# Two-layer graph attention kernel: the last graphs' logits with WX stationary, their Wh evicted in place, the adjacency cast in quarters, masks and small vectors in another order

## The chip, the cores and the metric

The kernel runs on one core of a Trainium2 chip. The metric is the device time of one execution in microseconds (us), start of the program to its end. The engines of a core work side by side and meet at semaphores: TensorE (PE in the profile, with its weight loads as PEld), VectorE (DVE), ScalarE (ACT), GpSimd (POOL) and SyncE (SP, which here only issues transfers). Transfers are issued from SP, ACT and POOL and carried by 16 DMA engines.

## The reference, cut to what matters

Sixteen graphs of 1024 nodes with 256 features pass through two layers. The first layer is the one that the change touches:

```python
Wh = einsum('bnf,of->bno', h, W)
ei, ej = Wh @ a1, Wh @ a2
att = ei[:, :, None] + ej[:, None, :]
att = bn(att, g1, b1)              # over graphs and columns, one mean and variance per row
att = where(att >= 0, att, 0.2 * att)
att = bn(att, g2, b2)
att = softmax(att, axis=2) * adj
h = elu(bn(att @ Wh, g3, b3))
x = layernorm(x + h)
```

The two norms over `att` need the logits `ei` and `ej` of all 16 graphs before any graph can be aggregated. The second layer (four heads of attention over the same adjacency, with residual and layernorm) is the same before and after.

## The kernel before

The first layer runs in three stages, called A, B and C below.

**Stage A (lines 275 to 399)** makes the logits of all graphs. `WX` holds W with ten more columns: two for the logits and eight for the second layer. A graph's x (1 MB) is loaded by SP, five graphs ahead (`XB = 5`). It is worked through in four items of two 128-row blocks. `turn` transposes an item on PE (four matmuls with the identity, line 314), and ACT copies the result to SBUF (line 324). `product` multiplies it with `WX`, the transposed x being the stationary operand (line 338). For the first ten graphs the product has 266 columns. It is evicted by DVE to `wx` (line 343, two buffers), `finish` stores it as `wh_dram` (line 350) and copies the logits out (lines 351 and 352). For the last six graphs (`LATE`), only the ten extra columns are made (`pe`), and the transposed x stays in SBUF in the buffers that will hold masks and Wh later (`room`, `held`). Their Wh is made in stage B.

**Stage B (lines 401 to 656)** computes the two norms' statistics. First comes a chain of small DVE operations with two column sums on PE and one power on POOL (lines 470 to 533), then the thresholds are spread over the partitions (`theta_rows`, line 457). For each graph, a loop then compares 1024 thresholds with eight columns of values (line 610 on DVE, line 614 on ACT), sums by matmul (line 633) and collects (`compared`, line 559). Beside it `late.make` works off the products left over, two or three 128-row blocks per graph (line 423). It evicts them to a `wx` of its own with two buffers (lines 428 and 430) and stores each graph when complete (line 432). SP's queue here carries these stores, the first mask (line 142, a transposing transfer of the bf16 adjacency into SBUF), the broadcast rows `eb` (line 250) and `wh` of graphs 0 and 1 (line 246), in this order of issue:

```python
late.make(2 + (b % 2 == 0), True)
if b == 3:
    mts[0] = mask(mpool, 0, "mt0")
if b == 9:
    queries(0)
    queries(1)
    for n in range(min(2, B)):
        load(n)
```

The second mask follows after the loop, once the held x are used up.

**Stage C (lines 661 to 802)** aggregates. `weights` makes a graph's attention weights in eight slices on ACT and DVE (lines 672 to 686), one graph ahead of PE, and `aggregate` multiplies them with Wh on PE (line 716).

The adjacency comes as f32 and is used as bf16. `Casts.behind` (line 93) has POOL copy one element of a given tile, which makes POOL wait until that tile is written, and then issues a cast of one whole graph from DRAM to DRAM (line 98). Two are released in stage A (behind the logits of graphs 1 and 5), three in the loop of stage B (behind the sums of graphs 1, 6 and 11), the other eleven in stage C.

The order on PE, ACT, DVE and SP is the program's own in stages A and B. In stage C a scheduler sets it, and the transfers that belong to later stages (`shifted1`, lines 201 and 202, which rewrites `W1s` shifted by one row, so that one transfer covers 127 rows) are issued as early as their dependences allow: these two stand in SP's queue right behind the first five loads of x.

Of the kernel before, what the change touches and what calls it, by code (L numbers as in the profile page):

```python
# [19 lines left out]
P = 128  # L20
# [7 lines left out]
def kernel(  # L28
# [57 lines left out]
    class Casts:  # L86


        def __init__(self):
            self.b = 0  # L90
            self.mark = cpool.tile([1, 1], F32, name="mark")

        def behind(self, data):
            if self.b == B:
                return
            tc.keep_in_program_order(nc.gpsimd.tensor_copy(self.mark, data))  # L96
            tc.keep_in_program_order(
                nc.gpsimd.dma_start(
                    adj16[self.b].rearrange("(k p) j -> p k j", p=P),
                    adj[self.b].rearrange("(k p) j -> p k j", p=P),  # L100
                )
            )
            self.b += 1
# [112 lines left out]
    with ExitStack() as l0:  # L216
# [19 lines left out]
        LATE = 6  # L236
        xw = spool.tile([P, K, B, 2 * H], F32, name="xw")
# [14 lines left out]
        def room():  # L252

            held = {}
            late = list(range(B - LATE, B))
            for n, of in enumerate((0, 4)):
# [6 lines left out]
            for n in range(2):  # L263
                t = epool.tile([P, K, F], F32, tag="wh", name=f"held_w{n}", bufs=2)
                held[late[2 + n]] = t.rearrange("p k (c n) -> p k c n", c=C)
# [9 lines left out]
        with tc.tile_pool(name="apool", bufs=1) as apool, tc.tile_pool(  # L275
# [4 lines left out]
            XB = 5  # L280
            KK = 2
            xin, xTs, wxs, pxs, pes = {}, {}, {}, {}, {}
# [5 lines left out]
            w0 = apool.tile([P, C, F], F32, name="w0")  # L288
            nc.scalar.dma_start(w0, W0.rearrange("(c p) f -> p c f", p=P))
# [15 lines left out]
            load_x(0)  # L305
            wbc = load1w(apool)
            for b in range(1, min(XB, B)):
                load_x(b)
# [17 lines left out]
            def product(b, kk):  # L326
                if kk == 0 and b in held:
                    pes[b] = aps_w.tile([P, K, FX - F], F32, tag="w", name=f"pe_{b}")
                elif kk == 0:
                    wxs[b] = apool.tile([P, K, FX], F32, tag="wx", name=f"wx_{b}", bufs=2)  # L330
                for k in range(KK):
                    n = kk * KK + k
                    if b in held:
                        pw, lo = pes[b][:, n], F
                    else:
                        pw, lo = aps_w.tile([P, FX], F32, tag="w", name=f"pw0_{b}_{n}"), 0
                    for fc in range(C):
                        nc.tensor.matmul(  # L338
                            pw, xTs[b, kk][:, k, fc, :], WX[:, fc, lo:FX],
                            start=(fc == 0), stop=(fc == C - 1),  # L340
                        )
                    if b not in held:
                        nc.vector.tensor_copy(wxs[b][:, n, :], pw)

            def finish(b):
# [7 lines left out]
                if b + XB < B:  # L353
                    load_x(b + XB)
                if b in (1, 5):
                    casts.behind(eT[0:1, b, 0, 0:1])
                if b == 1:
                    parameters1()
                if b == 4:
                    parameters1_made()  # L360
# [20 lines left out]
            turn(0, 0)  # L381
            turn(0, 1)
# [3 lines left out]
            items = [(b, kk) for b in range(B) for kk in range(K // KK)]  # L386
            for n, (b, kk) in enumerate(items):
                product(b, kk)
                if kk == K // KK - 1:
                    finish(b)  # L390
                if n + 2 < len(items):
                    turn(*items[n + 2])
                if n == 5:
                    pv = aps.tile([P, P], F32, tag="aps", name="pv_1")
                    nc.tensor.transpose(pv, rows[1], ident)
                    nc.vector.tensor_copy(vecs[:, NA:at], pv[:, NA:at])
            nc.sync.dma_start(
# [3 lines left out]
        with tc.tile_pool(name="bpool", bufs=1) as bpool, tc.tile_pool(  # L401
# [5 lines left out]
            class Late:  # L407


                def __init__(self):  # L410
                    self.n, self.wx = 0, None

                def make(self, count, shared):

                    for _ in range(count):
                        if self.n == LATE * K:
                            return
                        b, k = B - LATE + self.n // K, self.n % K
                        if k == 0:
                            self.wx = bpool.tile([P, K, F], F32, tag="wx", name=f"wx_{b}", bufs=2)  # L420
                        pw = bps_w.tile([P, F], F32, tag="w", name=f"pw0_{b}_{k}")
                        for fc in range(C):
# [3 lines left out]
                            )  # L426
                        if shared and self.n % 2:
                            nc.vector.tensor_copy(self.wx[:, k], pw)
                        else:
                            nc.scalar.copy(self.wx[:, k], pw)  # L430
                        if k == K - 1:
                            nc.sync.dma_start(wh_dram[b], self.wx)
# [102 lines left out]
            ths = {b: theta_rows(b) for b in range(min(NT, B))}  # L535
            to_rows(th_dram, theta.rearrange("p b k -> p (b k)"), "th")
            to_rows(ec_dram, ec.rearrange("p b k -> p (b k)"), "ec")

# [7 lines left out]
            rest = small(qpool, "rest", [B, K])  # L546
            for n, src in ((1, ec), (4, e2)):
                nc.vector.tensor_copy(powers[:, :, :, n], src)
                nc.vector.tensor_tensor(rest, src, powers[:, :, :, n], ALU.subtract)
                nc.vector.tensor_copy(powers[:, :, :, n + 1], rest)  # L550
                nc.vector.tensor_tensor(rest, rest, powers[:, :, :, n + 1], ALU.subtract)
                nc.vector.tensor_copy(powers[:, :, :, n + 2], rest)
            nc.vector.tensor_scalar(
                powers[:, :, KV:, :], powers[:, :, KV:, :], 0.5, None, ALU.mult
            )
# [3 lines left out]
            def compared(b):  # L559
# [7 lines left out]
                if b in (1, 6, 11):  # L567
                    casts.behind(sums[0:1, 0, 0, b : b + 1])

            t1 = small(qpool, "t1", [B])  # L570
            nc.vector.tensor_scalar(t1, p_mean, float(N), None, ALU.mult)
            t2 = small(qpool, "t2", [B])
            nc.vector.tensor_tensor(t2, p_mean, p_mean, ALU.mult)
# [1470 lines left out]
```

## Time and profile before

| | |
|---|---|
| time, median of 3 runs | 2304.25 us (2298.92 to 2311.9) |
| the profiled execution's own time | 2281.53 us |
| its span in the profile | 2279.8 us |
| PE busy | 2065.0 us (91% of the span) |
| DVE busy | 1823.9 us (80%) |
| ACT busy | 1454.4 us (64%) |
| granted TensorE clock, mean | 0.924 of full speed |

The profile shows one execution, 1% shorter than the median of the timed runs. The stages in it: A from 0 to 185 us, B to 313 us, where the first aggregation matmul starts, C to 821 us, the second layer after that. Some groups of instructions with count, busy time and mean duration of one (an fp32 matmul leaves two records, a transpose one):

```profile
L338 PE MATMUL pw<-WX,xT 128*128 128x266 f32 x320 | 82.7, 403 | 19.7 <-DVE wx L343 18.9 <-DVE WX L385 0.8
L314 PE MATMUL px<-ident,x 128*128 128x128 f32 x256 | 49.0, 326 | 0.0
L338 PE MATMUL pe<-WX,held_m 128*128 128x10 f32 x128 | 24.5, 324 | 0.0
L324 ACT COPY held_m<-px 128x512 f32<-128x512 f32 x16 | 9.4, 586 | 25.1 <-PE px L314 25.1
```

A matmul's duration in such a row includes the time in the pipeline, so a stretch of PE work is read from the starts in the timeline, not from these means.

### The profile page before, as it was taken

How to read it: one execution, taken by the hardware profiler on the slowest of the kernel's cores; microseconds unless marked ns; L12 is line 12 of the kernel's file. 1: busy time of each engine (PE TensorE's matmuls, PEld its weight loads, DVE VectorE, ACT ScalarE, POOL GpSimd, SP SyncE). 2: the span in 40 equal slices, each digit the busy share in tenths (PEclk: the TensorE clock that was granted, in tenths of full speed). 3: DMA queues.
4: the chain of work that ended last, by engine and by line, in shares of the span. 5: the costliest groups of instructions: out<-in, count | busy, mean ns of one | idle time of the engine just before them, and what ended most of it. 6: DMA issues, size and time to landing. Idle time of an engine off the chain costs nothing.

```text
span 2279.8 us, 36099 instructions
## 1 busy us (share of the span) xinstructions
PE 2065.0 (91%) x12248; PEld 1625.0 (71%) x12248; DVE 1823.9 (80%) x4468; ACT 1454.4 (64%) x3192; POOL 938.5 (41%) x1019
## 2 busy tenths in 40 slices
PE   5999677999999955999999999999999999999997
PEld 4798543444444423888888888887888888888886
DVE  2416588999999845789789889788898888898786
ACT  1225466777777613767767767767867857767775
POOL 1001000000000004767657667656667667667572
PEclk9967787999999975999999999999999999999998
DMA  7844968999995225756756746756756756756551
GB/s 210 251 162 131 256 141 180 227 223 228 233 237 143 100 84 170 223 163 169 207 154 166 216 157 167 210 156 162 212 165 166 212 162 164 202 175 164 122 160 42
DMA packets 321224, 403.14 MB, mean 177 GB/s; under 512 B 171089, under 2 KB 267397, under 8 KB 310021
## 3 DMA queue, kind: packets, MB, share of 16 engines
q1 hardware_dynamic: 269389, 254.73, 39.2%
q0 software_dynamic: 51072, 145.61, 26.0%
q8 instruction: 99, 1.62, 0.3%
q14 instruction: 96, 0.79, 0.1%
q10 hardware_dynamic: 568, 0.40, 0.1%
HBM read 329.32 MB, written 104.88 MB: 190 GB/s over the span
## 4 chain that ended last, share of the span: by engine, by line
PE 48%; DVE 19%; issue 17%; DMA 7%; POOL 4%; ACT 4%; SPq 1%; DVEq 0%; ACTq 0%; POOLq 0%
PE pa L716 12%; PE pv L1806 11%; PE pt L1783 8%; PE pu L1711 7%; PE po L1414 3%; POOL xc L1489 3%; DMA x<-in_x_dram 3%; PE pw L338 2%; DMA xc<-xe_dram,ix 2%; DVE d L610 2%; PE pz L1584 2%; DVE v L1814 1%; DVE w L1524 1%; DVE B L1375 1%; DVE w L1520 1%
## 5 line engine op out<-in xcount | busy, mean ns | idle before, releaser
L1489 POOL DMA_INDIRECT xc<-xe_dram,ix x640 | 682.5, 1066 | 212.0 <-issue 183.1
L1806 PE MATMUL pv<-W1s,sT 128*128 128x256 f32 x2048 | 506.1, 391 | 0.4 <-ACT sT L1800 0.4
L716 PE MATMUL pa<-em,wh 128*128 128x512 f32 x1024 | 450.5, 598 | 15.6 <-DVE em L680 15.6
L1806 PEld LDWEIGHTS pv<-W1s,sT 128*128 128x128 f32 x2048 | 382.0, 197 | 44.4 <-ACT sT L1800 0.8
L716 PEld LDWEIGHTS pa<-em,wh 128*128 128x128 f32 x1024 | 193.8, 192 | 248.0 <-issue 244.6
L1783 PEld LDWEIGHTS pt<-MX,s 125*128 125x128 f32 x2560 | 349.3, 203 | 29.7 <-ACT sT L1793 8.9
L1783 PE MATMUL pt<-MX,s 125*128 125x100 f32 x2560 | 350.1, 286 | 4.4 <-ACT sT L1793 2.0
L1711 PE MATMUL pu<-xc,w 128*125 128x256 f32 x1280 | 346.6, 390 | 0.5 <-ACT s L1777 0.5
L1820 ACT ACTIVATE m<-v,neg 128x512 f32<-128x512 f32 x256 | 183.7, 718 | 200.4 <-DVE v L1814 145.6
L1777 ACT ACTIVATE s<-pu,z 125x256 f32<-125x256 f32 x640 | 261.5, 474 | 76.2 <-DVE z L1769 50.1
L1711 PEld LDWEIGHTS pu<-xc,w 128*125 128x125 f32 x1280 | 232.3, 192 | 35.1 <-issue 5.7
L1793 ACT COPY sT<-pt 128x500 f32<-128x500 f32 x256 | 144.1, 563 | 111.9 <-PE pt L1783 111.9
L672 ACT ACTIVATE e<-eb,c,s 128x1024 f32<-128x1024 f32 x128 | 153.8, 1234 | 74.0 <-DVE sm L686 26.6
L1863 POOL TENSOR_TENSOR ors<-ors,mhalf 128x1 f32<-128x1 f32 x128 | 113.1, 883 | 207.2 <-DVE ors L1857 205.9
L1814 DVE TENSOR_TENSOR v<-pv,x 128x512 f32<-128x512 f32 x256 | 175.1, 684 | 14.9 <-PE pv L1806 14.5
L676 ACT ACTIVATE e<-e,v,u 128x1024 f32<-128x1024 f32 x128 | 152.6, 1231 | 26.2 <-DVE e L675 22.1
L680 DVE TENSOR_TENSOR em<-e,mt 128x1024 f32<-128x1024 f32 x128 | 155.2, 1221 | 4.6 <-ACT e L676 3.9
L675 DVE SCALAR_TENSOR_TENSOR e<-e 128x1024 f32<-128x1024 f32 x128 | 152.3, 1221 | 3.1 <-ACT e L672 3.1
L1584 PE MATMUL pz<-IW,h 128*128 128x136 f32 x512 | 90.2, 308 | 61.9 <-DVE fs L1601 37.7
L96 POOL COPY mark<-hb 1x1 f32<-1x1 f32 x11 | 2.8, 252 | 332.3 <-DVE sums L731 332.3
L1584 PEld LDWEIGHTS pz<-IW,h 128*128 128x128 f32 x512 | 77.3, 205 | 77.2 <-issue 44.0
L686 DVE TENSOR_TENSOR sm<-sm,e 128x1024 f32<-128x1024 f32 x96 | 117.4, 1223 | 1.2 <-ACT e L676 1.0
(323 smaller groups left out, 3300.0 us busy)
## 6 DMA issues: line engine op xcount, KB each, us to landing
x<-in_x_dram SPq DMA_DIRECT2D x32, 1024.0 KB
adj<-in_adj_dram POOLq DMA_DIRECT2D x16, 2048.0 KB
rw<-adj SPq DMA_DIRECT2D x32, 1024.0 KB
A<-u_dram SPq DMA_DIRECT2D x128, 250.0 KB
xe_dram<-x SPq DMA_DIRECT2D x16, 1060.0 KB
wh_dram<-wx SPq DMA_DIRECT2D x16, 1024.0 KB
wh<-wh_dram SPq DMA_DIRECT2D x16, 1024.0 KB
h_dram<-hb SPq DMA_DIRECT2D x16, 1024.0 KB
```

Source lines behind the costliest of these rows:

```text
L672: nc.scalar.activation(e, ebs[b], AF.Identity, bias=c1[:, k, b : b + 1], scale=s1[:, k : k + 1])
L676: nc.scalar.activation(e, e, AF.Exp, bias=v2[:, k : k + 1], scale=u2[:, k : k + 1])
L680: nc.vector.tensor_tensor(em, e, mts[b][:, k, :], ALU.mult)
L716: nc.tensor.matmul(acc[b, hf, oc].rearrange("p k q -> p q k"), wh[b][:, k, oc * P : (oc + 1) * P], ems[b, k][:, hf * HALF : (hf + 1) * HAL ...
L1489: nc.gpsimd.indirect_dma_start(out=self.xc[:, i, :], out_offset=None, in_=xe_dram[g.b % 2], in_offset=bass.IndirectOffsetOnAxis(ap=g.l.ix[ ...
L1584: nc.tensor.matmul(pz[:, oc, :], self.h[:, oc, k * P : (k + 1) * P], IW[:, oc, :], start=True, stop=True,)
L1711: nc.tensor.matmul(pu[0:QR, 0:F], c.w[:, k].rearrange("p h q -> p (h q)"), c.xc[:, k, 0:F], start=(i == 0), stop=(i == len(OF[q]) - 1),)
L1777: nc.scalar.mul(f.s[0:QR, i], f.pu[i][0:QR, 0:F], f.z[0:QR, i : i + 1])
L1783: nc.tensor.matmul(self.pt[:, :, :, i], self.first.s[0:QR, i, self.hp * P : (self.hp + 1) * P], MX[0:QR], start=True, stop=True,)
L1806: nc.tensor.matmul(self.pv[:, hh, :], self.first.sT[:, fc, self.hp * HP + hh, :], W1s[:, fc, self.hp * HP + hh, :], start=(fc == 0), stop= ...
L1814: nc.vector.tensor_tensor(self.v2, self.pv, self.g.x[:, self.it].unsqueeze(1).to_broadcast([P, HP, F]), ALU.add)
L1820: nc.scalar.activation(self.m, self.v2, AF.Exp, bias=neg1, scale=1.0)
```

## The change

1. **Late graphs' logits.** For the six late graphs `WX`'s ten columns become the stationary operand and 512 rows of transposed x stream past them: four fp32 matmuls per graph (`logits`). DVE copies the 10x512 result to SBUF twice per graph, and eight transposes per graph bring it back to rows (`turned_logits`), two items later.
2. **Order of graphs.** Stage A takes graphs 2 to 15 first and then 0 and 1 (`ORDER`), so the late ones are 12, 13, 14, 15, 0 and 1.
3. **Wh in place.** `late.make` evicts a product over the held x that it came from. There is no `wx` in stage B, graphs 0 and 1 are neither stored nor loaded again, and the held buffers are dealt out otherwise.
4. **`wx` in stage A** has three buffers instead of two.
5. **Casts in quarters.** `Casts.behind` casts 256 rows at a time. Nine quarters are released in stage A (one behind each of the first nine graphs), fifteen in the loop of stage B (one behind each graph's sums), four after graph 0 of stage C and four with each graph after that.
6. **Order in stage B.** Only graph 0's thresholds are spread ahead of the rows' stores. The powers and the moments of z are computed inside the loop. The masks are issued at graphs 4 and 10.
7. In stage A `W0` is loaded behind the small vectors `a1` and `a2`.

```diff
@@ Casts
         def behind(self, data):
-            if self.b == B:
+            b, part = divmod(self.n, 4)
+            if b == B:
                 return
             tc.keep_in_program_order(nc.gpsimd.tensor_copy(self.mark, data))
+            n = N // 4
+            rows = slice(part * n, (part + 1) * n)
             tc.keep_in_program_order(
                 nc.gpsimd.dma_start(
-                    adj16[self.b].rearrange("(k p) j -> p k j", p=P),
-                    adj[self.b].rearrange("(k p) j -> p k j", p=P),
+                    adj16[b][rows].rearrange("(k p) j -> p k j", p=P),
+                    adj[b][rows].rearrange("(k p) j -> p k j", p=P),
                 )
             )
...
+        ORDER = list(range(2, B)) + [0, 1]
...
@@ room
-            late = list(range(B - LATE, B))
-            for n, of in enumerate((0, 4)):
+            late = ORDER[B - LATE :]
+            for n, of in enumerate((0, 2)):
...
-                t = epool.tile([P, K, F], F32, tag="wh", name=f"held_w{n}", bufs=2)
-                held[late[2 + n]] = t.rearrange("p k (c n) -> p k c n", c=C)
+                t = wh[n] = epool.tile([P, K, F], F32, tag="wh", name=f"wh_{n}", bufs=2)
+                held[late[4 + n]] = t.rearrange("p k (c n) -> p k c n", c=C)
...
+            def logits(b, hf):
+                ps = aps_w.tile([OC, HALF], F32, tag="w", name=f"pl0_{b}_{hf}")
+                for fc in range(C):
+                    nc.tensor.matmul(
+                        ps, WX[:, fc, F:FX], held[b][:, hf * KH : (hf + 1) * KH, fc, :],
+                        start=(fc == 0), stop=(fc == C - 1),
+                    )
+                if hf == 0:
+                    els[b] = apool.tile([OC, N], F32, tag="el", name=f"el_{b}", bufs=2)
+                nc.vector.tensor_copy(els[b][:, hf * HALF : (hf + 1) * HALF], ps)
+
+            def turned_logits(b):
+                pe = pes[b] = aps.tile([P, K, OC], F32, tag="aps", name=f"pe_{b}")
+                for k in range(K):
+                    nc.tensor.transpose(
+                        pe[:, k], els[b][:, k * P : (k + 1) * P], ident[0:OC, 0:OC]
+                    )
...
@@ finish
-                if b in (1, 5):
+                if n < 9:
                     casts.behind(eT[0:1, b, 0, 0:1])
...
                 product(b, kk)
-                if kk == K // KK - 1:
-                    finish(b)
+                if b in held and kk % 2 == 1:
+                    logits(b, kk // 2)
+                if kk == KN - 1 and b not in held:
+                    finish(n // KN)
+                before = items[n - 2][0] if n >= 2 else None
+                if before in held and items[n - 2][1] == KN - 1:
+                    turned_logits(before)
+                    finish((n - 2) // KN)
                 if n + 2 < len(items):
                     turn(*items[n + 2])
...
@@ Late.make
+                        to = held[b][:, k].rearrange("p c n -> p (c n)")
                         if shared and self.n % 2:
-                            nc.vector.tensor_copy(self.wx[:, k], pw)
+                            nc.vector.tensor_copy(to, pw)
                         else:
-                            nc.scalar.copy(self.wx[:, k], pw)
-                        if k == K - 1:
-                            nc.sync.dma_start(wh_dram[b], self.wx)
+                            nc.scalar.copy(to, pw)
+                        if k == K - 1 and b > 1:
+                            nc.sync.dma_start(wh_dram[b], held[b].rearrange("p k c n -> p k (c n)"))
...
-            ths = {b: theta_rows(b) for b in range(min(NT, B))}
+            ths = {0: theta_rows(0)}
             to_rows(th_dram, theta.rearrange("p b k -> p (b k)"), "th")
             to_rows(ec_dram, ec.rearrange("p b k -> p (b k)"), "ec")
+            for b in range(1, min(NT, B)):
+                ths[b] = theta_rows(b)
...
-                if b in (1, 6, 11):
+                if b < 15:
                     casts.behind(sums[0:1, 0, 0, b : b + 1])
...
                 late.make(2 + (b % 2 == 0), True)
-                if b == 3:
+                if b == 4:
                     mts[0] = mask(mpool, 0, "mt0")
+                if b == 10:
+                    mts[1] = mask(mpool, 1, "mt0")
                 if b == 9:
                     queries(0)
                     queries(1)
-                    for n in range(min(2, B)):
-                        load(n)
...
@@ stage C
-                    if n == K + 4 and b > 0:
-                        casts.behind(hb[b][0:1, 0, 0:1])
+                    if n % 4 == 3 and b > 0:
+                        casts.behind(ems[b, k][0:1, 0:1])
```

## The prediction

> **What bounds the kernel now.** The page's second part comes first: which engine is full in which fortieth (57 us).
>
> ```profile
> PE   5999677999999955999999999999999999999997
> DVE  2416588999999845789789889788898888898786
> PEclk9967787999999975999999999999999999999998
> ```
>
> From the eighth slice on PE is full at full clock, but for the turn between the layers (slices 15 and 16). The first seven, stages A and B, are not, and all the edits but the cast's pacing lie there. Next, the busy times by window (columns: window, its length, busy PE, PEld, DVE, ACT, POOL, granted clock, DMA share, GB/s):
>
> ```profile
> 40.00:60.00 20.00, 3.61 (x21) 2.85 (x19) 0.00 (x0) 1.17 (x2) 0.61 (x1) 0.69 1.04 255
> 140.00:160.00 20.00, 20.00 (x100) 20.00 (x99) 0.61 (x4) 5.06 (x9) 0.00 (x0) 0.50 0.15 52
> 220.00:240.00 20.00, 19.50 (x371) 17.50 (x370) 20.00 (x47) 17.99 (x22) 4.74 (x7) 1.00 1.09 234
> 240.00:260.00 20.00, 11.19 (x155) 9.09 (x153) 6.42 (x16) 4.82 (x6) 0.08 (x1) 0.72 1.11 204
> 399.00:430.20 31.20, 31.19 (x92) 15.03 (x91) 29.48 (x33) 23.64 (x27) 1.85 (x2) 1.00 1.01 226
> ```
>
> At 40 us all stand and the DMA is full. At 140 PE works, at half clock. At 220 DVE is the bound of stage B's loop. At 240 all stand again. A graph of stage C takes 31.2 us with PE and DMA both full. The chain of waits names the two stalls (start, length, what):
>
> ```profile
> 39.49 0.63 SPq L202
> 40.21 20.30 DMA wh_dram<-wx
> 60.61 0.45 DVE wx L343
> ...
> 254.88 9.76 SPq L142
> 264.76 4.23 DMA wh_dram<-wx
> ```
>
> Both end with a store that frees a `wx` buffer. SP's timeline says why the stores were late:
>
> ```profile
> 19.04 21.08 SPq L202 DMA_DIRECT2D W1s<-in_L_gnn_W_dram  x1
> 219.15 45.49 SPq L142 DMA_TRANSPOSE mt<-adj  x1
> 264.76 0.97 SPq L432 DMA_DIRECT2D wh_dram<-wx  x2
> 265.79 2.35 SPq L250 DMA_DIRECT2D eb<-ec_dram  x2
> ```
>
> SP is held 21 us by a shift of W1s queued behind one that covers 127 rows, and 45 us by a mask; a mask's median over the 16 is 11.2 us.
>
> **Stage A, the stall at 40 us.** PE stops at 43.6, waits 17.6 us (61.19), then runs eight matmuls at half clock (3.73 us for 1.80): 1.9 more. A second wait at 118 costs 1.35. Sum 20.9. With three buffers PE may run one graph further, 8.96 us (four items of 0.44+1.80), to 52.5. But the first two quarters fall into the time in which the 127-row transfer moves 25 GB/s (24 to 40 us), about a sixteenth of the 380 GB/s that the same queue moves at 116 to 124. The Trainium skill, DMA: Bandwidth & Descriptors, "Why a DMA increments its semaphore by 16 and not by 1", says that 127 partitions put a transfer on one engine; the trace agrees. A quarter puts 16 packets of 0.18 us (below) on that engine too, 2.9 us each: SP is freed near 46 instead of 40.2, the store behind it lands near 53 to 55. I keep **3 us** of stall (ends 0 and 6). Afterwards the DMA holds the pace narrowly: 2 MB per graph at 380 GB/s are 5.4 us, a quarter 2.9, sum 8.3 of 8.96. Gain 20.9-3 = **18**.
>
> **Stage A, late graphs.** Before, from 131.6 to 184.9: 53.3 us, half clock from 136.3 on. After, per graph at full clock: 16 transposes at 0.11 = 1.76; the logits' 4 fp32 matmuls of 512 columns, 8 records at 0.43 (stage C's pace: 64 in 27.5 us) = 3.44; eight small transposes, bound by their weight loads as the 128x10 products are (0.10 each at full clock) = 0.8; twice a wait for ACT's copy (0.26 to start, 0.59, 0.05 back, less one turn of 0.44) = 0.92. Together 6.92, six times 41.5, less 0.9 for turns made earlier, plus 2.2 at the end (copy 0.95, eight transposes, two handovers): 42.8. DVE's 12 copies (bounds 0.43, the 128x266 copy, and 0.68, the 128x512 add) lie beside PE but for the last. Gain **10.5**, if the clock stays full. It does where enough streams: with ten columns streamed per load it fell to 0.50. Two cases decide:
>
> ```profile
> 876.97 3.57 PE L1678 MATMUL pX<-xs,ones 128*1 128x256 f32 x8 [0.21 <-DVE xs L1670]
> 877.00:880.40 3.40, 3.40 (x8) 0.82 (x8) 1.81 (x3) 2.21 (x6) 0.00 (x0) 0.50 0.96 322
> 880.40:883.80 3.40, 1.87 (x37) 1.39 (x36) 0.71 (x2) 3.15 (x5) 0.76 (x1) 1.00 0.22 40
> 197.75:201.16 3.41, 2.74 (x21) 1.88 (x19) 3.17 (x9) 2.91 (x6) 0.00 (x0) 1.00 0.49 197
> ```
>
> One stationary column streaming alone warmed the clock from 0.50 to 1.00, so ten columns count. The last row holds only transposes (theta's) and the clock stayed 1.00 after it. The Trainium skill, TensorE: Matmul & The Clock Gate, "Part 4: PE-mode transpose", says that a transpose doesn't count as PE being busy in the same way. By the rule only 3.44 of 6.92 us count; by the row 5.2. If the rule's reading led to half clock, a graph would take 12.2 us and the six 73: 31 us worse. I follow the row; the loop of stage B also keeps 1.00 with late products of 1.8 to 2.7 us in 4.
>
> **Stage B, start.** The sum of squares waits 1.9 us on PE (190.0), because two late products run at half clock ahead of it. With a warm PE: gain **1.7** (0 to 2).
>
> **Stage B, order of thresholds.** DVE starts comparing after th of graph 0, near 199 instead of 205, but idles 196.8 to 199 for it, and then does the same powers (4.5 us) and z moments (3.4) in a loop that DVE bounds. Loss **0.8** (-1 to +2.5).
>
> **Stage B, the stall at 246.** DVE waits 22.7 us for `wx`, and 1.0+2.0 more at 281.9 and 284.4 for a PE gone cold. In-place eviction needs no buffer: the copies are the same, nothing of PE, DVE or ACT waits for SP any more. Gain **25.7**.
>
> **Stage B, what is late next.** Behind the mask in SP's queue stand two stores and then `eb` of graph 0, which ACT needs for its first weight. A mask beside casts (225 to 234 us):
>
> ```profile
> q0 software_dynamic: 775, 1.59, 95.2%
> q1 hardware_dynamic: 696, 0.18, 15.1%
> ```
>
> About one packet of each in turn, 77 mask packets per us of 8192; alone (303 to 309) 6565 in 5.8 us. The same skill page, "Queues, rings and completion order", says that an engine goes round its queues packet by packet. This rule speaks against the change: cutting the casts does not help the mask, what counts is how long that queue is never empty, and the loop now releases 15 quarters where it had 12. Count from the loop's start (205 us before): POOL's queue holds 15 quarters at 2.97 us and eight th rows at 1.5, 57 us, with 5 for SP's transfers between; its last quarter is released near 66 and ends near 71. The mask starts near 19, gets 52 us at 77 (4000 packets), about 3 us of gaps (3400) and the rest after: done near 72. Two stores at 2.7, the row 1.6 and its latency: `eb` lands near 80. The loop ends near 68. By the row of before (45 us from start to SP's release, all then as it was) it would land near 74; were casts and mask to share evenly, before 68. I take **12 us** of delay (0 to 16). The instruction order of the changed kernel makes it whole: DVE's first weight now stands ahead of thirteen of the moments' operations and the power on POOL, so all of that queues behind `eb`. The first masked weight then comes 13.7 after `eb`, against 13.9 after the loop's end before (312.0-298.1). The second mask, issued next and alone on the DMA, lands some 24 us before its use: no cost.
>
> **Stage C.** Per graph the same instructions. Graphs 0 and 1 lose load and store, both hidden. Four marks instead of one are POOL's, idle otherwise. Casts end after graph 9 instead of 10. **0** (-2 to +8).
>
> **Sum:** 18+10.5+1.7-0.8+25.7-12 = 43.1. From the profiled execution's 2281.5: **2238**. The runs shown have a median 22.7 above it, and I take the same distance: **2261**.
>
> **Rivals.**
> - `eb` is not late, because gaps between quarters let the mask through: 12 more, 2249. For it: the mask that met no cast took 8.0 us. Against: 57+5 us of work in 65.
> - The late part runs at half clock, should ten columns or transposes count for little: 43-31 = 12 gained, 2292.
> - The first stall stays in part: should the first store land at 60.5 as before, PE with its third buffer still waits 60.5+0.6-52.5 = 8.6 and pays 1.9 for the cold clock: 10.4 gained there instead of 18, 2269. For it: two quarters on the slow engine; against: the cast then taking the DMA is a quarter, not the whole.
> - Slower: starved masks in stage C. From graph 1 on three of four quarters are released by the same last weight that frees the mask's buffer. I reckon 3 quarters (8.9 us) in turn with a load and then 8 us alone: near 19 us of 31. If a mask is held as the first was, 45 us, PE waits about 20 in each of nine graphs: 180-43, about 2440. It decides from a mask of about 26 us on. Against it: casts have some 4 us of start on the mask.
>
> **How the numbers follow.** Chances: forecast 0.60, `eb` in time 0.23, half clock 0.05, first stall in part 0.08, starved masks 0.04. The forecast's own bounds (stall 3, late part 3, `eb` 5, stage C 5, the runs' spread 6) give about 16 either way; with the neighbours 2236 to 2286. A difference of 0.5%, 11.5 us, is about what these runs tell from none. Faster 0.93, same 0.03, slower 0.04.
>
> **What would show it.** Right: no wait of PE on `wx` over 6 us in stage A, clock 1.00 between 112 and 155, its end near 157; no DVE wait for a store in stage B; the first mask over 45 us long on SP, and ACT's first weight waiting on `eb` for about 12 us. Wrong: clock 0.50 in the late part, a mask under 40 us, or PE idle inside stage C.

## The result and the profile after

The changed kernel takes **2283.89 us** (median of 20 runs, 2269.28 to 2307.3) beside 2306.02 us for the kernel before (20 runs, 2295.89 to 2322.17): a ratio of 0.990 with a 95% interval of 0.9876 to 0.9924. That is faster by some 22 us, where 43 were forecast. The sign was right, and the time lies in the stated range, which ended at 2286, by 2 us only: it is outside the forecast's own 16 us around 2261, and inside because the range took in the neighbouring cases, none of which came. Half of the sum is missing. (A run over 1.5% longer than the fastest of its kernel is left out of the ratios but not of the medians: two of the 20 here, three of 22 in e6, one of six in e11 and four of six in e4, whose ratio therefore says little.)

The two profiled executions hide even this. Their spans are 2279.8 before and 2277.4 after, a difference of only 2.4 us. Laid side by side, the first aggregation matmul starts at 313.3 before and at 290.7 after (22.6 us earlier), the last one at 819.5 and 796.0 (23.5 earlier), and then the second layer, of which no line differs, takes 1460 before and 1481 after. So the gain of the timed runs is all there when the first layer ends; what eats it afterwards has to be looked at by itself (first experiment). First the stages A and B. From part 2 of the page after the change:

```profile
PE   6989269999999935999999999999999999999996
DVE  3439398999999554689889789889898898898885
PEclk9999679999999955999999999999999999999998
```

The clock, six to eight tenths in the slices three to seven before, is now full in the first four. PE's fifth to seventh slices had six, seven and seven tenths before; now one deep hole stands in the fifth, 228 to 285 us, where PE is busy for two tenths. The windows show both (columns: window, its length, busy PE, PEld, DVE, ACT, POOL, granted clock, DMA share, GB/s):

```profile
132.00:148.00 16.00, 14.80 (x82) 7.23 (x82) 4.05 (x11) 5.10 (x10) 0.00 (x0) 1.00 0.00 0
247.50:290.70 43.20, 0.00 (x0) 0.02 (x1) 9.82 (x27) 7.22 (x7) 1.68 (x1) 0.50 1.08 187
```

The first is the late graphs' part, at clock 1.00 where it was 0.50. In the second PE does nothing for 43.2 us, while the DMA is full. The page's group of the aggregation says who ends this wait (last columns: idle time before, and by whom):

```profile
L752 PE MATMUL pa<-em,wh 128*128 128x512 f32 x1024 | 450.4, 598 | 43.6 <-DVE em L716 43.6
```

The same group before:

```profile
L716 PE MATMUL pa<-em,wh 128*128 128x512 f32 x1024 | 450.5, 598 | 15.6 <-DVE em L680 15.6
```

The chain of waits leads back from DVE's `em` (start, length, what):

```profile
247.12 19.72 SPq L145
...
267.98 9.35 DMA eb<-ec_dram
...
277.43 1.25 ACT e L708
...
289.38 2.36 DVE em L716 x2
```

This is the wait that the prediction named, `eb` behind the mask in SP's queue, at more than twice its size. SP's timeline has the mask:

```profile
195.70 71.13 SPq L145 DMA_TRANSPOSE mt<-adj  x1
266.95 0.97 SPq L462 DMA_DIRECT2D wh_dram<-held_m  x2
267.98 2.34 SPq L254 DMA_DIRECT2D eb<-ec_dram  x2
```

71 us instead of 45 before. The DMA of two short windows tells how it ends (queue, packets, MB, share of the 16 engines; q0 carries the casts, q1 what SP issues):

```profile
q0 software_dynamic: 349, 0.68, 74.7%
q1 hardware_dynamic: 523, 0.13, 46.7%
```

```profile
q1 hardware_dynamic: 322, 0.08, 133.1%
q0 software_dynamic: 14, 0.03, 6.3%
```

The first is 240 to 248 us: 65 mask packets per us. The second is 261.2 to 263.6: only 14 packets of the casts start, each 0.17 us long and 0.18 us after the last, as one engine would work them off one after the other (the trace does not say which engine carries a packet). Yet the mask gets only 134 packets per us, with all engines' time taken by packets that wait. In the trace the last cast packet starts at 266.5, and SP is free at 266.8.

### The profile page after: what moved, and what is told of

Same layout as the page of the kernel before. It is cut to its first block, busy times and chain, and to the rows that moved or that the text cites. A ratio compares the mean times of both kernels' runs of the same rounds, so it can differ in the third digit from the quotient of the medians.

```text
span 2277.4 us, 36056 instructions
## 1 busy us (share of the span) xinstructions
PE 2043.3 (90%) x12152; PEld 1587.2 (70%) x12152; DVE 1831.2 (80%) x4480; ACT 1454.9 (64%) x3192; POOL 1005.0 (44%) x1115
## 4 chain that ended last, share of the span: by engine, by line
PE 60%; DVE 21%; ACT 7%; issue 4%; DMA 4%; POOL 1%; SPq 1%; another core or an unknown queue 0%; DVEq 0%; ACTq 0%; POOLq 0%
PE pa L752 18%; PE pv L1843 11%; PE pt L1820 8%; PE pu L1748 8%; PE po L1451 3%; PE pw L340 2%; PE pz L1621 2%; DVE v L1851 2%; DVE w L1561 1%; ACT s L1814 1%; DVE B L1412 1%; DVE w L1557 1%; PE pd L729 1%; DMA xc<-xe_dram,ix 1%; DVE w L1565 1%
## 5 line engine op out<-in xcount | busy, mean ns | idle before, releaser
L752 PE MATMUL pa<-em,wh 128*128 128x512 f32 x1024 | 450.4, 598 | 43.6 <-DVE em L716 43.6
L711 DVE SCALAR_TENSOR_TENSOR e<-e 128x1024 f32<-128x1024 f32 x128 | 152.1, 1218 | 30.1 <-ACT e L708 30.1
L97 POOL COPY mark<-em 1x1 f32<-1x1 f32 x36 | 32.0, 889 | 187.8 <-DVE mn L771 97.0
```

Source lines behind the costliest of these rows:

```text
L752: nc.tensor.matmul(acc[b, hf, oc].rearrange("p k q -> p q k"), wh[b][:, k, oc * P : (oc + 1) * P], ems[b, k][:, hf * HALF : (hf + 1) * HAL ...
```

## The experiments

All runs in one table. "Mask" is the time for which the first mask holds SP; "gap" is from the start of the loop's last collecting copy on DVE to the first aggregation matmul, with that matmul's start; C is from the first to the last aggregation matmul; "layer 2" from there to the end. The last four columns are of one profiled execution each, the ratio is of the timed runs to the kernel before on the same chip.

| run | time, us | ratio (95%) | mask | gap, first pa | C | layer 2 |
|---|---|---|---|---|---|---|
| before, first profile | 2306.0 | | 45.5 | 15.6, 313.3 | 506 | 1460 |
| after, first profile | 2283.9 | 0.990 (0.9876 to 0.9924) | 71.1 | 43.6, 290.7 | 505 | 1481 |
| e1 before again | 2304.6 | 1.000 (0.998 to 1.002) | 47.8 | 15.2, 314.8 | 506 | 1494 |
| e2 eb first | 2250.8 | 0.977 (0.974 to 0.980) | 71.0 | 27.1, 277.6 | 514 | 1486 |
| e3 casts later | 2263.1 | 0.983 (0.979 to 0.987) | 37.2 | 13.6, 268.0 | 508 | 1469 |
| e4 fours | 2299.5 | 0.984 (0.979 to 0.989), two of six runs | 64.7 | 43.9, 297.4 | 532 | 1476 |
| e5 mask alone | 2257.7 | 0.984 (0.978 to 0.990) | 8.7 | 13.6, 258.3 | 505 | 1492 |
| e6 C marks | 2295.1 | 0.995 (0.993 to 0.998) | 78.5 | 51.7, 312.3 | 505 | 1484 |
| e7 old logits | 2311.7, one run | none | 64.9 | 37.1, 307.8 | 511 | 1491 |
| e8 wx two | 2297.6, one run | none | 66.7 | 38.9, 296.0 | 506 | 1494 |
| e9 best | 2224.7 | 0.974 (0.971 to 0.977) | 8.5 | 13.6, 259.4 | 505 | 1460 |
| e10 after again | 2260.6 | 0.990 (0.985 to 0.994) | 68.7 | 42.2, 287.2 | 512 | 1462 |
| e11 C one by one | 2258.6 | 0.979 (0.976 to 0.983) | 9.3 | 13.6, 259.3 | 505 | 1484 |
| e12 best again | 2254.7 | 0.978 (0.974 to 0.982) | 8.7 | 13.6, 260.4 | 505 | 1493 |

The kernel before took 2304 to 2306 on the chips of e1 to e8, e11 and e12, but 2283.4 (11 runs, 2277.2 to 2294.8) on that of e9 and e10. Times are therefore compared by their ratios.

**e1: the kernel before, once more.**

> The kernel before, unchanged. In its first profile the second layer (from the last aggregation matmul to the end) took 1460.3 us, in the changed kernel's profile 1481.4, though no line of the second layer differs. Theory: the first profile of before was a fortunate execution of the second layer; another one shows 1475 to 1485 there and an own time near the median of 2306, while the first aggregation matmul again starts near 313. Rival: the change costs the second layer some 20 us (code or data placed differently); then this profile shows 1460 again.

Its own time was 2316.7, its median 2304.6. The first aggregation matmul starts at 314.8 (313.3 in the first profile) and the second layer takes 1493.5. So the theory holds, and a little beyond its numbers: the 21 us by which the second layer seemed to lose are no cost of the change. e9 and e10 point to the chip: on theirs it took 1460 and 1462, on the others 1469 to 1494. On which chip the first profile of before was taken is not on record; its 2281.5 lies among the times of before on the chip of e9 and e10 and below all of those on the others (from 2285.2 on). On that chip the changed kernel beats the kernel before by 22.8 us (2260.6 and 2283.4), as in the first comparison.

**e2: `eb` ahead of the mask.** Only the place of two loads in SP's queue differs:

```diff
+                if b == 3:
+                    queries(0)
+                    queries(1)
                 if b == 4:
                     mts[0] = mask(mpool, 0, "mt0")
...
-                if b == 9:
-                    queries(0)
-                    queries(1)
```

> The changed kernel, with the loads of eb for graphs 0 and 1 issued one loop step ahead of the first mask on SP instead of behind it. Theory (eb is late because SP is held by the mask): eb lands before 215, ACT forms the first weights right after the loop's end near 247, and what is late next is the mask itself (it ended at 267): the first aggregation matmul starts near 269 instead of 290.7, 20 to 22 us earlier, time near 2263. Rival (the DMA as a whole is full, and whatever is put ahead pushes the rest back): less than 8 us gained.

`eb` is no longer waited for; now it is the mask, as the line of DVE's timeline shows (idle time and its end in brackets):

```profile
276.28 2.36 DVE L716 TENSOR_TENSOR em<-e,mt 128x1024 f32<-128x1024 f32 x2 [14.84 <-DMA mt<-adj]
```

The first aggregation matmul starts at 277.6, 13 us earlier instead of 20 to 22: I had taken the moment at which SP is free for the landing of the mask. In the changed kernel the mask's last packet starts 1.5 us after that moment (268.4), but here SP is free at 264.2 and DVE gets the mask 12 us later. The cause that was named is right, but it has two parts, and moving `eb` removes only one. The timed runs gain more than the profile: 0.977 against 0.990. Of its six times four are 2250 to 2251, and the profiled one is the slowest (2279.7), with a wait of 8.5 us in graph 9 of stage C. So its trace does not explain its median; that stays open.

**e3: the casts later.**

```diff
-                if b < 15:
+                if b < 4:
                     casts.behind(sums[0:1, 0, 0, b : b + 1])
...
-                    if n % 4 == 3 and b > 0:
+                    if b == 0 and n < 11 or n % 4 == 3 and b > 0:
                         casts.behind(ems[b, k][0:1, 0:1])
```

> The changed kernel, with 4 instead of 15 quarters of casts released in the loop of stage B, and the 11 others behind the masked weights of graph 0 in stage C. Theory (the casts starve the mask): the mask takes at most 16 us instead of 71, eb lands before 235, the first aggregation matmul starts about 15 us after the loop's end, near 262 instead of 290.7; stage C and its end are as late after that as in the changed kernel: 26 to 30 us gained, time near 2256. Rival (the casts' work only moves and holds up the masks of stage C): masks of 30 us and more there, PE idle in graphs 1 to 3, and less than 10 us gained.

The gap is 13.6 us, the very length of the chain without any wait for a transfer, and the median is 2263.1. But the mask took 37.2 us, not 16, and the first aggregation matmul starts at 268.0 instead of the expected 262. The rival, masks of 30 us and more in stage C, did not come: the longest took 25.6 us and cost PE 2.3. By count, 2.6 quarters and six of the rows passed beside the first mask. In the window 214 to 220 no cast is under way any more, only rows of thresholds that POOL also issues on q0:

```profile
q1 hardware_dynamic: 1033, 0.26, 95.8%
q0 software_dynamic: 60, 0.22, 32.3%
```

60 packets of q0 in 6 us hold the mask to 172 packets per us. In the trace some of these took 1.4 to 2.0 us instead of 0.16. That the mask packets of all engines then go in step with the slowest fits this rate; no view shows it engine by engine.

**e4: as much as before, four quarters at a time.**

```diff
-                if b < 15:
+                for _ in range(4 if b in (1, 6, 11) else 0):
                     casts.behind(sums[0:1, 0, 0, b : b + 1])
```

> The changed kernel, with 12 quarters in the loop of stage B, released four at a time at the three steps at which the kernel before released a whole cast, instead of 15 one by one. Theory (what counts is how much is cast and how long that queue is never empty, not the cut into quarters): the mask takes 45 to 55 us as before, eb lands near 258, first aggregation matmul near 271: 15 to 22 us gained. Rival (cutting the casts in quarters is itself what slows the mask): the mask stays over 65 us and nothing is gained.

The mask took 64.7 us and the gap is 43.9: what was expected of the theory did not come. In the kernel before, the third cast of the loop was released at 281.4, after its mask was done at 264.6; only two whole casts fell beside the mask. Here all twelve quarters were released by 239.1, and the mask, which starts 27 us after the loop's first comparison instead of 15, lay beside the last eight and what was left of the first four. I had counted casts in the loop, where casts beside the mask decide. Yet by count these are nearly equal: 8.9 quarters and six rows here, 8.0 and six before, and still the mask took 64.7 us instead of 45.5. The queue of the casts moved 42 packets per us here from 214 to 250, but 82 before from 225 to 255. So the amount alone does not set the mask's time, and this speaks for the rival; it does not prove it, since the releases also lie at other times. What the end of the drain shows is unevenness: the mask's last packet starts at 273.0 with 1.2 quarters still to come, and from 279 to 282, with the mask gone and the DMA busy for 45%, the casts' queue moves only 64 packets, which take 20.6% of the engines' time, as if three or four of the 16 engines held all that was left. The profiled execution also lost 26 us in graph 10 of stage C, to a mask that took 43 us. The ratio of 0.984 comes from the two shortest of its six times; the median of all six is 0.997 of before's.

**e5: nothing in the casts' queue beside the mask.**

```diff
-                if b < 15:
+                if b in (12, 13, 14):
                     casts.behind(sums[0:1, 0, 0, b : b + 1])
...
                 if b + 8 < B:
-                    load_th(b + 8, nc.gpsimd)
+                    load_th(b + 8, nc.sync)
...
-                    if n % 4 == 3 and b > 0:
+                    if b == 0 and n < 12 or n % 4 == 3 and b > 0:
                         casts.behind(ems[b, k][0:1, 0:1])
```

> The changed kernel, with the queue of the casts left empty while the first mask runs: the rows of thresholds 8 to 15 go by SP instead of POOL, no cast is released in loop steps 0 to 11 of stage B, three quarters are released in steps 12 to 14 and twelve behind the masked weights of graph 0. Theory (the mask goes one packet in turn with whatever stands in that queue on the slowest of the 16 engines, thresholds' rows included, so it is over only once the queue has drained everywhere): where the run with 4 quarters and 8 rows beside it still took 37 us, the mask now takes at most 14 us; eb lands before 230, the first aggregation matmul starts about 14 us after the loop's end and no later than 263; 25 us or more gained on the changed kernel. Rival (the mask is slow because of the full DMA of this stretch, whichever queue fills it): a mask of 25 us or more again, and a gain no larger than that run's 21 us.

SP's timeline, and the DMA from 198 to 207.5 us:

```profile
196.92 8.73 SPq L145 DMA_TRANSPOSE mt<-adj  x1
```

```profile
q1 hardware_dynamic: 8316, 2.42, 116.3%
```

8.7 us instead of 71.1, and the first aggregation matmul at 258.3 instead of 290.7. The rival falls: the DMA is as full (116% beside 108%), and 2.4 MB pass in the 9.5 us, but in one queue. The gain over the changed kernel is 32.4 us in the trace; the median is 2257.7 on a chip where before took 2304.2. The intervals of the two ratios, 0.984 and 0.990, still overlap, so the size of this gain rests on the traces.

**e6: stage C's casts released as before.**

```diff
-                    if n % 4 == 3 and b > 0:
-                        casts.behind(ems[b, k][0:1, 0:1])
+                    for _ in range(4 if n == K + 4 and b > 0 else 0):
+                        casts.behind(hb[b][0:1, 0, 0:1])
```

> The changed kernel, with the casts of stage C released as before, all four quarters of a graph behind hb (step 12 of 16), instead of one by one behind masked weights. In the changed kernel's stage C three quarters start with the mask, the masks took 17 to 19 us, one 27 us, and in two other profiles PE stood 8 and 26 us in graph 9 or 10. Theory (a part of the missing gain is paid there, in some executions): masks of 10 to 13 us, 30.1 us for every graph from 3 on, and a median 3 to 10 us below the changed kernel's 2283.9 with fewer times above 2295. Rival (stage C costs the changed kernel nothing): the same time within 3 us.

From graph 4 on the masks of stage C are 10 to 14 us again, and each graph takes 28.4 to 30.5, as before. But the time did not fall, it is 2295.1 (0.995). In the profile everything is lost in stage B, which this edit does not touch: the mask takes 78.5 us, the gap is 51.7, and PE stands twice inside the loop, for 9.7 us and once more for 3.1:

```profile
221.77 0.54 PE L670 MATMUL pt<-powers,d 128*128 128x7 bf16 x15 [9.73 <-issue]
```

The DMA of 212 to 221 us has one transfer of code in it (16 KB, "instruction"):

```profile
q8 instruction: 1, 0.02, 4.0%
```

4.0% of 16 engines over 9 us are 5.8 us for one packet that takes 0.9 to 1.3 in most other places. So the gain expected of stage C is not shown, and why these 22 runs lie 0.5% behind the changed kernel's ratio stays open.

**e7: the late logits as before.** `product` makes the ten columns of a late graph against its transposed x again, and `logits` and `turned_logits` are no longer called:

```diff
-                if b in held:
-                    return
-                if kk == 0:
+                if kk == 0 and b in held:
+                    pes[b] = aps_w.tile([P, K, OC], F32, tag="w", name=f"pe_{b}")
+                elif kk == 0:
...
+                    if b in held:
+                        pw, lo = pes[b][:, n], F
...
-                            pw, xTs[b, kk][:, k, fc, :], WX[:, fc, :],
+                            pw, xTs[b, kk][:, k, fc, :], WX[:, fc, lo:FX],
```

> The changed kernel, with the late graphs' logits made as before: ten columns streamed against the transposed x as stationary. Theory (the gain of this part is the clock's): half clock again in the late part, which takes 52 to 54 us instead of 40.1, and stage A ends 13 us later, near 170. Rival (the half clock before came from something else, such as the DMA stall's end or the transposes): the late part stays at full clock and, with half of before's 8.9 us per graph, is over in some 27 us, earlier than in the changed kernel.

```profile
132.00:148.00 16.00, 16.00 (x81) 16.00 (x81) 0.61 (x4) 4.10 (x7) 0.00 (x0) 0.50 0.00 1
```

Half clock again, where the new form had 1.00 in the same window with about as many instructions. The first comparison of the loop starts at 178.8 instead of 169.6, 9 us later, not 13: the first 10 us of the part still ran at full clock, and the part took 48.4 us, not 52 to 54 (41.3 in the changed kernel). The theory holds: this part's gain is the clock's.

**e8: two buffers of `wx`.**

```diff
-                    wxs[b] = apool.tile([P, K, FX], F32, tag="wx", name=f"wx_{b}", bufs=3)
+                    wxs[b] = apool.tile([P, K, FX], F32, tag="wx", name=f"wx_{b}", bufs=2)
```

> The changed kernel, with two instead of three buffers of wx. In the changed kernel the first store landed at 56.3 us and PE, started 5 us later than before because W0 came later, reached its third graph's end at about the same time, so it hardly waited. Theory: with two buffers PE stands from about 47.5 until 57, 9 us, and works 2 us more at half clock; the late part starts near 127 instead of 116.5. Rival (the quarter of a cast in place of the whole one is what removed the stall): the late part starts before 120.

PE's timelines of e8, of the changed kernel and of e9 (below), in this order:

```profile
57.09 3.67 PE L340 MATMUL pw<-WX,xT 128*128 128x266 f32 x8 [10.20 <-DVE wx L344]
```

```profile
56.98 2.04 PE L340 MATMUL pw<-WX,xT 128*128 128x266 f32 x8 [0.52 <-DVE wx L344]
```

```profile
57.65 3.88 PE L340 MATMUL pw<-WX,xT 128*128 128x266 f32 x8 [5.69 <-DVE wx L344]
```

With two buffers PE waits 10.2 us and is at half clock after it; the first logits of the late graphs come at 126.7 instead of 117.1, and the loop starts 9.5 us later. All three waits end with the landing of the first graph's store, at 56.3 to 57.0.

**e9: the version put together:** e5, with stage C's casts as in e6, and W0's load first on ACT's queue.

```diff
+            w0 = apool.tile([P, C, F], F32, name="w0")
+            nc.scalar.dma_start(w0, W0.rearrange("(c p) f -> p c f", p=P))
             rows = [apool.tile([P, P], F32, name=f"rows_{i}") for i in range(2)]
```

> The run with the first mask alone, and besides: all four quarters of a graph in stage C released behind hb as before, and W0's load put first on ACT's queue again, ahead of the rows of a1 and a2. Theory: the first product starts near 18.2 instead of 23; PE has then three graphs done near 51 and waits for the store that lands near 56, so that the late part begins no more than 1.5 us earlier than the 116.5 of the changed kernel; mask 0 under 14 us, first aggregation matmul near 257, masks of stage C 10 to 14 us and no PE wait there: time 2250 to 2260, with fewer high times than the run before it. Rival (the late W0 is a loss of its own): the late part begins 5 us earlier, and the time falls by 5 us more.

The first product starts at 18.7 instead of 23.2, and PE gives the 5 us back at 52 to 57.7 (the third line above); the late graphs' first logits come at 119.3 instead of 117.1. So the later W0 of the changed kernel costs nothing. The time is 2224.7 at a ratio of 0.974, with five runs within 2.4 us of each other; that it is below the expected 2250 to 2260 is mostly the chip, on which before too is 21 us shorter.

**e10: the changed kernel again, on that chip.**

> The changed kernel, unchanged, timed beside the others and profiled once more. Theory (its first mask takes 65 to 79 us in every execution and lands between 268 and 288): the first aggregation matmul starts 37 to 52 us after the loop's end, between 290 and 312; time near 2284 to 2290. Rival (the first profile's 71 us was a bad execution): a mask under 55 us, as predicted, and a first aggregation matmul before 280.

Mask 68.7 us, gap 42.2, first aggregation matmul at 287.2 (expected from 290 on): the long mask is no accident of the first profile. The ratio is 0.990 again. This execution also shows stage C's weak place, in SP's and in DVE's timeline:

```profile
553.24 27.31 SPq L145 DMA_TRANSPOSE mt<-adj  x1
```

```profile
589.08 1.23 DVE L716 TENSOR_TENSOR em<-e,mt 128x1024 f32<-128x1024 f32 x1 [4.97 <-DMA mt<-adj]
```

A mask of 27.3 us, and graph 9 takes 36.0 instead of 30.1 on PE.

**e11 and e12: stage C's release once more, on one chip.** e11 is e9 with the changed kernel's release in stage C (the opposite of e6's diff), e12 is e9 itself.

> The best version so far, with stage C's casts released as in the changed kernel again (one quarter behind every fourth masked weight) instead of four behind hb. Theory (this release lets masks of stage C take 17 to 31 us and PE wait for one of them around graph 9 in some executions, 0 to 26 us in eight profiles so far): masks of 17 us and more in graphs 3 to 9, a median 3 to 12 us above the best version's on the same chip, and times that scatter by 15 us or more where the best version's scatter by less than 5. Rival (stage C's release costs nothing, as the changed kernel's first profile has it): the same median within 2 us and the same scatter.

> The best version once more, on the same chip as the run with the other release in stage C: a ratio to the kernel before of 0.971 to 0.977 again, times within 5 us of each other, and PE's 30.1 us for every graph of stage C from the fourth on.

Masks of 17 to 30 us in e11's graphs and of 10 to 13 in e12's later ones, but C is 505 us in both. The medians are 4 us apart with overlapping intervals, and e12's times scatter by 19 us, not 5 (e11's by 54). e12's ratio of 0.978 is just beyond the expected 0.977. The order of the two is as expected, but it is not shown that the release costs time.

## Why the prediction was right in sign and half in size

| step | forecast | measured in the two first profiles |
|---|---|---|
| stage A up to the late part | +18 | +15.1 (131.6 to 116.5) |
| late graphs, to DVE's copy of the last logits | +10.5 | +11.8 (53.1 to 41.3) |
| start of B, order, stall at 246 | +26.6 | +23.7 (113.0 to 89.3) |
| what is late next (`eb`) | -12 | -28.0 (gap 15.6 to 43.6) |
| sum at the first aggregation matmul | 43.1 | 22.6 |

**Stage A.** The wait on `wx` is gone but for 0.5 and 0.9 us; I kept 3. This was right partly by luck: I overlooked that W0's load, moved behind the rows of a1 and a2, makes the first product 5.0 us late (18.2 to 23.2). The same store that bounds the third buffer hides this: e8 and e9 show PE held to about 57 us whichever way it comes there. Without the slip the stall would have kept 5.7 us and a cold clock, more than my 3.

**Late graphs.** Mechanism and size held. The clock was 1.00 throughout, stage A ended at 157.8 (forecast near 157), and e7 brings the half clock back with the old form. The clock went the way of the row; whether transposes count is not told apart by it, because the logits' 3.44 us of streaming per graph may be enough by themselves.

**Stage B.** No DVE wait for a store is left, so the 25.7 us went as said. What is short by 2.9 us is about what PE lost inside the loop, where it stood 2.93 us with no releaser that the profile shows, and worked at half clock after it:

```profile
242.75 0.76 PE L670 MATMUL pt<-powers,d 128*128 128x7 bf16 x23 [2.93 <-issue]
```

A 16 KB packet of code, which takes 0.9 to 1.3 us in most other places, took 2.9 us in the trace from 238.4 on. The kernel before had such a pause of 3.2 us (5.4 in e1), but inside the stall that went. e2, e3, e4, e6 and e7 have it with 5.7 to 11.5 us, e8 with 3.7, e10 with 1.7; e5, e9, e11 and e12, with the mask alone, do not have it. In the ten profiles that have it there are twelve such pauses, and in each of them PE goes on 1.3 to 1.6 us after a 16 KB packet of code has ended. So that it waits for code is well supported by the packets' times; no run shows it by itself. In none of the steps did I ask what a starved DMA does to the engines' own code. The Trainium skill, Runtime: NRT & Kernel Launch, "Instruction fetch mechanics", calls the crossing of a 16 KB block mostly hidden; beside a full DMA it was not here, if the packets' times are read rightly.

**What is late next: this is the step that failed, by its size.** The prediction said that the mask's queue of casts would be empty when "its last quarter is released near 66 and ends near 71", and `eb` would land near 80, counted from 205 us in the trace before. Less the 30.2 us that the forecast gains ahead of that point (18+10.5+1.7), these are 240.8, 245.8 and 254.8. Measured are 244.3, 266.5 and 277.4. The release was 3.5 us late, and from there to the end of the casts it took 22 us instead of 5. The term behind it is the price of a quarter. I took 2.97 us, the pace of the casts beside the mask in the row of before (775 packets in 9 us, 256 to a quarter), and kept it to the end. The changed kernel's queue does keep it at first, with 88 packets per us from 205 to 225, but from 240 to 248 it moves 44, and the 846 cast packets that start after the last release, 3.3 quarters, took 22 us, 6.7 us each.

That casts and mask go one packet each in turn, which the prediction took from the row and from the Trainium skill (DMA: Bandwidth & Descriptors, "Queues, rings and completion order"), fits the stretch from 205 to 225: 1757 packets of the casts' queue and 1788 of the mask's. As an average over 16 engines it misleads. The counts of the end of the mask fit engines that do not finish together, with a mask that advances in step with the slowest (e4's casts, which trickle on after their mask is done, fit this too); while this lasts casts, mask and code loads all run far below their rate. That the packets in the other queue are the cause, e5 shows by removing them (8.7 us), e3 in part (37.2, with the thresholds' rows still in that queue), and e2 shows that both `eb` and the mask itself hang on it. That the amount alone decides, e4 refutes. Why the casts lose their pace when cut in quarters, and kept it as whole casts, stays open.

**Stage C and the rivals.** C was put at 0 (-2 to +8): it gained 0.9 in the first profile and lost 6.1 in e10. The slower rival, masks starved in stage C with a price from about 26 us on, is real in some executions: masks of 25 to 30 us gave waits of 0 to 5.9, 31 us gave 8.5, 43 us gave 26. But it strikes one graph out of sixteen, not nine. The mask that lies beside three quarters mostly takes 17 to 20 us, as reckoned (19). The half clock and the first stall did not come, nor did `eb` in time.

**The offset to the median** (22.7 us) was the first profile's chip or execution, as e1 shows, and it was carried over unchanged. The median missed by 22.9 us, 20.5 of which are the shortfall of the sum.

## What to carry to other kernels

Before a long transposing transfer is put into a queue, list what other queues hold during its whole time: in these traces it was held until little was left of it, at most 2.7 quarters (e4, e6, e7) and otherwise next to nothing, and everything behind it in its own queue waited as long. Moving the casts away from the mask's time and the small rows into the mask's own queue took it from 71 to 9 us and brought 32 us in the trace, more than the rest of the change together. When a stall is removed, ask not only who is late next, but whether the work that the stall had kept apart now falls together.

## What the runs showed of the hardware that was not expected

- A transposing transfer of 8192 packets of 256 B held SP for 8.5 to 9.3 us with the casts' queue empty, for 45 to 48 beside two whole casts and six rows (before, e1), and for 65 to 79 beside nine to thirteen quarters and six rows.
- SP is free some us before the mask has landed: 12 us in e2.
- PE stood 1.7 to 11.5 us in a straight stretch of code, with no releaser shown, where a 16 KB packet of code came late or took up to 5.7 us beside such transfers; it takes 0.9 to 1.3 us in most other places. It went on 1.3 to 1.6 us after the packet's end each time.
- The same second layer took 1460 and 1462 us on one chip (e9, e10) and 1469 to 1494 on three others (e1 to e8, e11 and e12). A single profiled span can hide a gain of 22 us.
